# Two blocks of j per instruction in the pairwise loop of a hyperbolic graph layer: load, mask, second gelu and both vector products widened, node features read from the summing table

## The chip, the cores and the metric

One core of a Trainium2 chip. The metric is the device time of one execution, in microseconds (us). Each version is run several times in rounds with the kernel before on the same chip. Engines in the profile: PE is TensorE's matmuls, PEld its weight loads, DVE is VectorE, ACT is ScalarE, POOL is GpSimd, SP the engine that issues the loads.

## The reference, cut to what matters

There are 3327 nodes with 64 features and a dense 0/1 adjacency matrix of 3327 x 3327 (44 MB in float32).

```python
h = relu(layernorm(x))
# layer 0, hyperbolic attention; c = 1 / r**2
x_t     = logmap0(h, c)
adj_att = sigmoid((x_t @ w_l)[:, None] + (x_t @ w_r)[None, :] + b) * adj
x_local = logmap(h[:, None, :], h[None, :, :], c)        # every pair of nodes
support = einsum('ij,ijd->id', adj_att, x_local)
x = x + proj(expmap(h, support, c), c)
# layer 1: weights that decay with the rank of a neighbour in its row
h = relu(layernorm(x))
rank = cumsum(adj != 0, axis=1); ...                     # cut
x = x + w @ (h @ weight) + bias
```

For the argument it is enough that layer 0 needs for each pair (i, j) a sigmoid, a scalar function of a "distance", and their product with adj, summed over j with the features of j. Layer 1 needs how many neighbours of i lie behind j.

## The kernel before

The columns i are cut into four strips of 8, 8, 6 and 4 blocks of 128 (1024, 1024, 768 and 512 wide). Within a strip a loop runs over the 26 blocks of j, from the last to the first. This is its body, with comments added; `V` is VectorE, `A` ScalarE, `T` TensorE.

```python
for j in range(NB - 1, -1, -1):
    ad = work.tile([P, FMAX], F32, name="ad", bufs=4)
    nc.sync.dma_start(ad[:, :F], adj_t[j * P : (j + 1) * P, i0 : i0 + F])
    mask = work.tile([P, FMAX], BF16, name="mask", bufs=3)
    V.tensor_scalar(mask[:, :F], ad[:, :F], 0.0, None, op0=ALU.not_equal)        # mask
    for f0, f1 in hv:                                                            # counts, into ONE bank pc
        if not first:
            T.matmul(pc[:, f0:f1], ca, before[:, f0:f1], ...)
        T.matmul(pc[:, f0:f1], cb, mask[:, f0:f1], ...)
    before = mask
    ...                                                                          # count copy: pc -> uint8,
    if j % (2 if b0 == 0 else 4): A.activation(kept, counts, AF.Relu)            # on ScalarE
    else:                         V.tensor_scalar(kept, counts, 0.0, None, op0=ALU.max)   # or VectorE

    sg = work.tile([P, FMAX], F32, name="sg", bufs=3)
    A.activation(sg[:, :F], left_b[:, :F], AF.Tanh, bias=right[:, j : j + 1], scale=0.5)
    V.scalar_tensor_tensor(sg[:, :F], sg[:, :F], 1.0, ad[:, :F], ...)            # product "sg"

    pq = ps.tile([P, FMAX], F32, name="pq", bufs=2)
    for f0, f1 in hv:                                                            # distances
        T.matmul(pq[:, f0:f1], ju[:KB, j, :], iuf[:, f0:f1], start=True, stop=False)
        T.matmul(pq[:, f0:f1], jz[:, j, :], izf[:, f0:f1], start=False, stop=True)
    s = work.tile([P, FMAX], F32, name="s", bufs=3)
    A.activation(s[:, :F], pq[:, :F], AF.Gelu, scale=-WG / QS)                   # first gelu
    A.activation(s[:, :F], s[:, :F], AF.Gelu, scale=WH)                          # second gelu
    V.scalar_tensor_tensor(s[:, :F], s[:, :F], WD, sg[:, :F], ...)               # product "s"
    for f0, f1 in hv:                                                            # the sum, four passes
        T.matmul(po[: D + 1, f0:f1], hw[:, j, :], s[:, f0:f1], start=first, stop=last)
    next(steps, None)                  # one step of the previous strip's closing arithmetic
```

After the last block of j a VectorE copy takes `po` out; this copy marks the strip's end below. The closing arithmetic of a strip (some 70 instructions, most of them 128 x 8) is spread over the next strip's loop. A scheduler at compile time fixes each engine's order of instructions. In PSUM, where this program puts its matmul results, it keeps two `pq`, one `pc` and one `po`.

The features of a node are kept twice: as `h`, and weighted, as `hw`, the summing table.

## Time and profile before

| | before |
|---|---|
| time | 484.36 us median of 3 runs (482.84 to 486.17) |
| span of the profiled execution | 483.4 us, mean granted clock 0.946 |
| strips end at (start of the closing copy) | 145.14, 250.15, 333.19, 394.20 us |
| busy | TensorE 82%, VectorE 86%, ScalarE 75% of the span |

A page of the profile has, among others, a line for the chain of work that ended last (shares of the span by engine) and lines for the costliest groups of instructions: line, engine, operation, output and inputs, count, then busy time and mean duration in ns, then the engine's idle time just before them with what ended most of it. The page of the kernel before:

```profile
DVE 54%; PE 22%; ACT 11%; issue 8%; DMA 3%; POOL 1%; DVEq 0%; ACTq 0%; POOLq 0%
...
L831 DVE SCALAR_TENSOR_TENSOR sg<-sg,ad 128x1024 f32<-128x1024 f32 (+2 forms) x104 | 105.6, 1019 | 7.5 <-ACT sg L830 7.3
L840 DVE SCALAR_TENSOR_TENSOR s<-s,sg 128x1024 f32<-128x1024 f32 (+2 forms) x104 | 106.2, 1021 | 5.3 <-ACT s L839 5.2
```

The two products, 104 of each, are half of VectorE's work, and VectorE carries half of the chain. The view of waits over 55 to 250 us (the full part of strips 1 and 2) has for each consumer the releaser, the total in us, how often, and the longest. For the count bank `pc` the kernel before has, among others, these three:

```profile
ACT behind_hi L824 <- PE pc L819: 5.7, 3, 4.5
...
ACT behind_lo L824 <- PE pc L819: 2.1, 3, 1.5
...
PE pc L818 <- ACT behind_lo L824: 1.1, 2, 0.9
```

TensorE waits 1.1 us in all for ScalarE's count copies in nearly 200 us.

### The profile page before, as it was taken

The page shows a single profiled execution, that of the slowest core. Times are in us where ns is not written, and L with a number is a line of the kernel's source. Part 1 is how long each engine was busy: PE and PEld are TensorE (multiplying, and loading weights), DVE is VectorE, ACT ScalarE, POOL GpSimd, SP SyncE. Part 2 cuts the span into 40 slices and gives each one's busy share as a digit, 9 for nine tenths or more (in the row PEclk, how much of TensorE's full clock was granted, in tenths as well). Part 3 has the DMA queues.
Part 4 walks back from the last instruction along what each step waited for, and adds up shares of the span by engine and source line. Part 5 has one row for each costly group of instructions (what it writes and reads, how often), then busy time and mean ns, then how long its engine had stood idle before and what let it go on. Part 6 is the DMA issues. An engine that isn't in the chain of part 4 may idle for free.

```text
span 483.4 us, 4793 instructions
## 1 busy us (share of the span) xinstructions
PE 396.6 (82%) x1484; PEld 159.0 (33%) x1484; DVE 413.6 (86%) x834; ACT 363.7 (75%) x446; POOL 14.0 (3%) x30
## 2 busy tenths in 40 slices
PE   0267799999997999998988988898899859974773
PEld 0035233333323333332333444343222214432432
DVE  3893779999988899999989999999999999997110
ACT  1345989999868999999959999995999966640000
POOL 5000000000000000001000000100000100000000
PEclk9999999999999999999999999999999997997555
DMA  7102445444451445343433453442453300000010
GB/s 208 42 10 58 135 130 170 138 163 135 130 155 45 137 149 158 122 138 123 130 105 104 147 142 109 121 120 65 116 147 110 108 2 0 0 1 1 22 32 24
DMA packets 23051, 47.79 MB, mean 99 GB/s; under 512 B 8861, under 2 KB 9291, under 8 KB 23017
## 3 DMA queue, kind: packets, MB, share of 16 engines
q1 hardware_dynamic: 20730, 46.47, 33.0%
q10 hardware_dynamic: 2062, 0.87, 0.9%
q0 software_dynamic: 224, 0.07, 0.3%
q8 instruction: 13, 0.21, 0.2%
q14 instruction: 22, 0.17, 0.1%
HBM read 45.22 MB, written 0.85 MB: 95 GB/s over the span
## 4 chain that ended last, share of the span: by engine, by line
DVE 54%; PE 22%; ACT 11%; issue 8%; DMA 3%; POOL 1%; DVEq 0%; ACTq 0%; POOLq 0%
DVE s L840 12%; PE po L842 10%; DVE sg L831 9%; DVE mask L815 6%; DVE wt L879 3%; DVE wt L880 3%; PE pw L907 3%; DVE behind_lo L826 3%; ACT s L839 2%; ACT s L838 2%; PE pw L884 2%; DMA w_lr<-in_w_att 2%; PE pc L818 2%; ACT sg L830 2%; PE pc L819 2%
## 5 line engine op out<-in xcount | busy, mean ns | idle before, releaser
L842 PE MATMUL po<-s,hw 128*65 128x512 f32 (+1 forms) x364 | 168.7, 581 | 12.4 <-DVE s L840 12.0
L831 DVE SCALAR_TENSOR_TENSOR sg<-sg,ad 128x1024 f32<-128x1024 f32 (+2 forms) x104 | 105.6, 1019 | 7.5 <-ACT sg L830 7.3
L840 DVE SCALAR_TENSOR_TENSOR s<-s,sg 128x1024 f32<-128x1024 f32 (+2 forms) x104 | 106.2, 1021 | 5.3 <-ACT s L839 5.2
L830 ACT ACTIVATE sg<-left_b,right 128x1024 f32<-128x1024 f32 (+2 forms) x104 | 103.6, 1000 | 0.3 <-DVE s L840 0.2
L839 ACT ACTIVATE s<-s 128x1024 f32<-128x1024 f32 (+2 forms) x104 | 94.1, 906 | 0.2
L838 ACT ACTIVATE s<-pq 128x1024 f32<-128x1024 f32 (+2 forms) x104 | 90.0, 870 | 3.8 <-PE pq L836 3.5
L835 PE MATMUL pq<-iu,ju 71*128 71x512 f16 (+1 forms) x182 | 68.1, 375 | 11.6 <-ACT s L838 11.4
L818 PE MATMUL pc<-mask,ca 128*128 128x512 bf16 (+1 forms) x175 | 65.2, 373 | 15.1 <-DVE behind_hi L826 6.7
L842 PEld LDWEIGHTS po<-s,hw 128*65 128x65 f32 x364 | 44.2, 138 | 100.4 <-DVE s L840 50.3
L819 PE MATMUL pc<-mask,cb 128*128 128x512 bf16 (+1 forms) x182 | 66.7, 376 | 5.7 <-DVE mask L815 5.5
L836 PE MATMUL pq<-iz,jz 128*128 128x512 f16 (+1 forms) x182 | 67.4, 375 | 0.0
L815 DVE TENSOR_SCALAR mask<-ad 128x1024 bf16<-128x1024 f32 (+2 forms) x104 | 61.0, 589 | 4.8 <-PE pc L818 2.9
L884 PE MATMUL pw<-wt,s 128*128 128x512 bf16 (+1 forms) x182 | 46.8, 413 | 16.4 <-DVE wt L880 5.5
L824 ACT ACTIVATE behind_hi<-pc 128x1024 uint8<-128x1024 f32 (+2 forms) x37 | 31.9, 861 | 25.5 <-PE pc L819 25.3
L819 PEld LDWEIGHTS <-cb 128*128 128x128 bf16 x182 | 17.9, 99 | 55.7 <-issue 44.6
L884 PEld LDWEIGHTS <-s 128*128 128x128 f16 x182 | 19.9, 110 | 38.5 <-issue 19.5
L824 ACT ACTIVATE behind_lo<-pc 128x1024 uint8<-128x1024 f32 (+2 forms) x33 | 28.2, 856 | 3.8 <-PE pc L819 3.2
L836 PEld LDWEIGHTS <-jz 128*128 128x128 f16 x182 | 18.2, 100 | 33.3 <-issue 18.1
L818 PEld LDWEIGHTS <-ca 128*128 128x128 bf16 x175 | 17.5, 100 | 31.3 <-issue 20.4
L835 PEld LDWEIGHTS <-ju 71*128 71x128 f16 x182 | 18.2, 100 | 23.9 <-issue 8.6
L902 ACT COPY ow<-pw 128x512 f32<-128x512 f32 x3 | 1.8, 586 | 30.8 <-PE pw L884 30.8
L909 DVE TENSOR_TENSOR o<-pw,x_sb 128x256 f32<-128x256 f32 (+1 forms) x7 | 2.8, 406 | 21.8 <-PE pw L907 21.8
(211 smaller groups left out, 325.6 us busy)
## 6 DMA issues: line engine op xcount, KB each, us to landing
ad<-in_adj_t SPq DMA_DIRECT2D x52, 512.0 KB, 3.6
ad<-in_adj_t SPq DMA_DIRECT2D x26, 384.0 KB, 3.2
ad<-in_adj_t SPq DMA_DIRECT2D x26, 256.0 KB, 2.8
out<-o SPq DMA_DIRECT2D x6, 128.0 KB, 2.0
x_sb<-in_x ACTq DMA_DIRECT2D x1, 416.0 KB
x_sb<-in_x SPq DMA_DIRECT2D x1, 416.0 KB
iz<-jz ACTq DMA_DIRECT2D x2, 128.0 KB
iz<-jz SPq DMA_DIRECT2D x2, 128.0 KB, 3.2
```

What stands on the lines that cost most here:

```text
L815: V.tensor_scalar(mask[:, :F], ad[:, :F], 0.0, None, op0=ALU.not_equal)
L818: T.matmul(pc[:, f0:f1], ca, before[:, f0:f1], start=False, stop=True, skip_group_check=True)
L819: T.matmul(pc[:, f0:f1], cb, mask[:, f0:f1], start=False, stop=True, skip_group_check=True)
L830: A.activation(sg[:, :F], left_b[:, :F], AF.Tanh, bias=right[:, j : j + 1], scale=0.5)
L831: V.scalar_tensor_tensor(sg[:, :F], sg[:, :F], 1.0, ad[:, :F], op0=ALU.add, op1=ALU.mult)
L835: T.matmul(pq[:, f0:f1], ju[:KB, j, :], iuf[:, f0:f1], start=True, stop=False)
L836: T.matmul(pq[:, f0:f1], jz[:, j, :], izf[:, f0:f1], start=False, stop=True)
L838: A.activation(s[:, :F], pq[:, :F], AF.Gelu, scale=-WG / QS)
L839: A.activation(s[:, :F], s[:, :F], AF.Gelu, scale=WH)
L840: V.scalar_tensor_tensor(s[:, :F], s[:, :F], WD, sg[:, :F], op0=ALU.add, op1=ALU.mult)
L842: T.matmul(po[: D + 1, f0:f1], hw[:, j, :], s[:, f0:f1], start=first, stop=last)
L884: T.matmul(pw[:, f0:f1], s2[:, j].rearrange("p c d -> p (c d)"), wt[:, f0:f1].bitcast(BF16), start=j == 0, stop=j == NB - 1)
```

## The change

The intent is to pay the fixed part of four kinds of instruction once per two blocks of j. In the kernel before this part is 0.07 us of the start-to-start time of a mask (0.60 us) and of a product (1.14), and 0.09 us of a second gelu's 0.95 (which lasts 0.639 us for 512 elements and 1.067 for 1024, so that 1024 elements cost 0.856). The loop steps by pairs of blocks: one load of 1 MB instead of two of 512 KB, one mask, one product sg, one second gelu, one product s. Tanh, first gelu, counts and all matmuls stay per block. The buffers keep four blocks of `ad` (two pairs), and get four instead of three of `mask`, `sg` and `s`. The table `h` goes; the closing arithmetic reads `hw` and multiplies by the factor `unw` that undoes the weight.

```diff
-    h = const.tile([P, NB, D], F32, name="h")
...
-        V.tensor_mul(h, rl, wide(y, NB))
+        V.tensor_scalar(unw, babs, 2.0 / WA, None, op0=ALU.mult)
...
-        hs, v, xs = h[:, bs], agg[:, :, :D], x_sb[:, bs]
+        hs, v, xs = hw[:, bs, :D], agg[:, :, :D], x_sb[:, bs]
...    (three small multiplications by unw[:, bs] are added in the closing arithmetic)
-        for j in range(NB - 1, -1, -1):
...    (the body shown above)
+        for j0 in range(NB - 2, -1, -2):
+            ad = work.tile([P, 2, FMAX], F32, name="ad")
+            nc.sync.dma_start(ad[:, :, :F],
+                              adj_t[j0 * P : (j0 + 2) * P, i0 : i0 + F].rearrange("(t p) f -> p t f", p=P))
+            mask = work.tile([P, 2, FMAX], BF16, name="mask")
+            V.tensor_scalar(mask[:, :, :F], ad[:, :, :F], 0.0, None, op0=ALU.not_equal)
+
+            sg = work.tile([P, 2, FMAX], F32, name="sg")
+            s = work.tile([P, 2, FMAX], F32, name="s")
+            for t in (1, 0):
+                j = j0 + t
...    (counts and count copy of block j)
+                A.activation(sg[:, t, :F], left_b[:, :F], AF.Tanh, bias=right[:, j : j + 1], scale=0.5)
...    (distances of block j)
+                A.activation(s[:, t, :F], pq[:, :F], AF.Gelu, scale=-WG / QS)
+            V.scalar_tensor_tensor(sg[:, :, :F], sg[:, :, :F], 1.0, ad[:, :, :F], op0=ALU.add, op1=ALU.mult)
+            A.activation(s[:, :, :F], s[:, :, :F], AF.Gelu, scale=WH)
+            V.scalar_tensor_tensor(s[:, :, :F], s[:, :, :F], WD, sg[:, :, :F], op0=ALU.add, op1=ALU.mult)
+            for t in (1, 0):
+                j = j0 + t
+                for f0, f1 in hv:
+                    T.matmul(po[: D + 1, f0:f1], hw[:, j, :], s[:, t, f0:f1], start=j == NB - 1, stop=j == 0)
+                next(steps, None)
```

More of the change, by code (lines that the diff above doesn't have):

```diff
@@ L515, in wide @@
         return t[:, :, None].to_broadcast([P, n, D])
-    h = const.tile([P, NB, D], F32, name="h")
-    x2, bal, balm, nrm, left, right = (
-        const.tile([P, NB], F32, name=n) for n in ("x2", "bal", "balm", "nrm", "left", "right"))
+    x2, bal, balm, nrm, left, right, unw = (
+        const.tile([P, NB], F32, name=n) for n in ("x2", "bal", "balm", "nrm", "left", "right", "unw"))
     hw = const.tile([P, NB, D + 1], F32, name="hw")
@@ L707, in post @@
         V.tensor_reduce(xy, dt, AX.X, ALU.add)
+        V.tensor_mul(xy, xy, unw[:, bs])
         V.scalar_tensor_tensor(sa, xy, m2c, agg[:, :, D], op0=ALU.mult, op1=ALU.add)
@@ L712, in post @@
         yield
-        V.tensor_mul(w, hs, wide(sa, nb))
+        V.tensor_mul(k, sa, unw[:, bs])
+        V.tensor_mul(w, hs, wide(k, nb))
         yield
@@ L747, in post @@
         yield
+        V.tensor_mul(t0, t0, unw[:, bs])
         V.tensor_mul(w, hs, wide(t0, nb))
@@ L809, in fast @@
         before = None
-        for j in range(NB - 1, -1, -1):
-            first, last = j == NB - 1, j == 0
-            ad = work.tile([P, FMAX], F32, name="ad", bufs=4)
-            nc.sync.dma_start(ad[:, :F], adj_t[j * P : (j + 1) * P, i0 : i0 + F])
-            mask = work.tile([P, FMAX], BF16, name="mask", bufs=3)
-            V.tensor_scalar(mask[:, :F], ad[:, :F], 0.0, None, op0=ALU.not_equal)
-            for f0, f1 in hv:
-                if not first:
-                    T.matmul(pc[:, f0:f1], ca, before[:, f0:f1], start=False, stop=True, skip_group_check=True)
-                T.matmul(pc[:, f0:f1], cb, mask[:, f0:f1], start=False, stop=True, skip_group_check=True)
-            before = mask
-            kept = behind(j)[:, i0 : i0 + F].rearrange("p (k q t) -> p k t q", t=2, q=P)
-            counts = pc[:, :F].rearrange("p (k t q) -> p k t q", t=2, q=P)
-            if j % (2 if b0 == 0 else 4):
-                A.activation(kept, counts, AF.Relu)
-            else:
-                V.tensor_scalar(kept, counts, 0.0, None, op0=ALU.max)
-            sg = work.tile([P, FMAX], F32, name="sg", bufs=3)
-            A.activation(sg[:, :F], left_b[:, :F], AF.Tanh, bias=right[:, j : j + 1], scale=0.5)
-            V.scalar_tensor_tensor(sg[:, :F], sg[:, :F], 1.0, ad[:, :F], op0=ALU.add, op1=ALU.mult)
-            pq = ps.tile([P, FMAX], F32, name="pq", bufs=2)
-            for f0, f1 in hv:
-                T.matmul(pq[:, f0:f1], ju[:KB, j, :], iuf[:, f0:f1], start=True, stop=False)
-                T.matmul(pq[:, f0:f1], jz[:, j, :], izf[:, f0:f1], start=False, stop=True)
-            s = work.tile([P, FMAX], F32, name="s", bufs=3)
-            A.activation(s[:, :F], pq[:, :F], AF.Gelu, scale=-WG / QS)
-            A.activation(s[:, :F], s[:, :F], AF.Gelu, scale=WH)
-            V.scalar_tensor_tensor(s[:, :F], s[:, :F], WD, sg[:, :F], op0=ALU.add, op1=ALU.mult)
-            for f0, f1 in hv:
-                T.matmul(po[: D + 1, f0:f1], hw[:, j, :], s[:, f0:f1], start=first, stop=last)
-            next(steps, None)
@@ new lines, in fast @@
+        for j0 in range(NB - 2, -1, -2):
[9 more added lines that the diff above has]
+                for f0, f1 in hv:
+                    if before is not None:
+                        T.matmul(pc[:, f0:f1], ca, before[:, f0:f1], start=False, stop=True, skip_group_check=True)
+                    T.matmul(pc[:, f0:f1], cb, mask[:, t, f0:f1], start=False, stop=True, skip_group_check=True)
+                before = mask[:, t]
+                kept = behind(j)[:, i0 : i0 + F].rearrange("p (k q t) -> p k t q", t=2, q=P)
+                counts = pc[:, :F].rearrange("p (k t q) -> p k t q", t=2, q=P)
+                if j % (2 if b0 == 0 else 4):
+                    A.activation(kept, counts, AF.Relu)
+                else:
+                    V.tensor_scalar(kept, counts, 0.0, None, op0=ALU.max)
+                A.activation(sg[:, t, :F], left_b[:, :F], AF.Tanh, bias=right[:, j : j + 1], scale=0.5)
+                pq = ps.tile([P, FMAX], F32, name="pq", bufs=2)
+                for f0, f1 in hv:
+                    T.matmul(pq[:, f0:f1], ju[:KB, j, :], iuf[:, f0:f1], start=True, stop=False)
+                    T.matmul(pq[:, f0:f1], jz[:, j, :], izf[:, f0:f1], start=False, stop=True)
+                A.activation(s[:, t, :F], pq[:, :F], AF.Gelu, scale=-WG / QS)
[4 more added lines that the diff above has]
+                j = j0 + t
+                for f0, f1 in hv:
+                    T.matmul(po[: D + 1, f0:f1], hw[:, j, :], s[:, t, f0:f1], start=j == NB - 1, stop=j == 0)
+                next(steps, None)
@@ L844, in fast @@
         for _ in steps:
             pass
-        ot = work.tile([P, FMAX], F32, name="s", bufs=3)[: D + 1]
+        ot = work.tile([P, 2, FMAX], F32, name="s")[: D + 1, 0]
         V.tensor_copy(ot[:, :F], po[: D + 1, :F])
```

## The prediction

> **What bounds the kernel now.** I read the stages first. The copy that closes each column strip (line L848) starts at 145.14, 250.15, 333.19 and 394.20 us, so I cut the span near those times and asked for the busy time of each engine in each stretch. The columns are the stretch, its length, then busy time and instruction count of PE, PEld, DVE, ACT and POOL, then the clock, the DMA share and GB/s.
> ```profile
> 48.00:146.00 98.00, 92.40 (x293) 32.20 (x291) 88.70 (x89) 87.56 (x91) 0.00 (x0) 1.00 0.47 143
> 146.00:251.00 105.00, 97.47 (x330) 34.79 (x331) 101.35 (x176) 97.66 (x106) 2.19 (x1) 0.98 0.43 128
> 251.00:332.00 81.00, 72.15 (x319) 33.25 (x319) 78.81 (x166) 76.38 (x105) 2.39 (x1) 1.00 0.42 118
> 332.00:395.00 63.00, 53.67 (x171) 16.41 (x170) 60.28 (x169) 55.37 (x105) 1.73 (x1) 1.00 0.35 95
> ```
> The first strip is bound by nothing alone: TensorE 94% of it, VectorE 91%, ScalarE 89%. In strips 2 to 4 VectorE is the fullest (97%, 97%, 96%), because it also does the previous strip's closing arithmetic. Before 48 us is a preamble that is a chain of small steps, after 395 us a tail that the change hardly touches. DMA is under half busy everywhere.
>
> Next I read the timeline for what one instruction really costs in a full queue. In the lines below the first number is the start, the second the duration.
> ```profile
> 240.62 1.21 DVE L840 SCALAR_TENSOR_TENSOR s<-s,sg 128x1024 f32<-128x1024 f32 x1
> 241.76 1.21 DVE L831 SCALAR_TENSOR_TENSOR sg<-sg,ad 128x1024 f32<-128x1024 f32 x1
> 242.90 0.68 DVE L815 TENSOR_SCALAR mask<-ad 128x1024 bf16<-128x1024 f32 x1
> 243.50 1.21 DVE L831 SCALAR_TENSOR_TENSOR sg<-sg,ad 128x1024 f32<-128x1024 f32 x1
> ```
> The durations overlap: from start to start a product takes 1.14 us and a mask 0.60 us. By form, the product at 128x512 lasts 0.684 us and at 128x1024 1.217 us, so 512 elements cost 0.533 us, and 1024 cost 1.066 us. The fixed part that merging can remove is therefore 1.14 - 1.066 = 0.07 us per instruction, not the 0.15 us that the durations suggest. The mask gives the same 0.07 (0.60 less half of 1.066).
>
> ScalarE and TensorE in the same way:
> ```profile
> 149.94 1.03 ACT L838 ACTIVATE s<-pq 128x1024 f32<-128x1024 f32 x1
> 150.85 1.15 ACT L830 ACTIVATE sg<-left_b,right 128x1024 f32<-128x1024 f32 x1
> 151.89 1.06 ACT L839 ACTIVATE s<-s 128x1024 f32<-128x1024 f32 x1
> 152.84 1.15 ACT L830 ACTIVATE sg<-left_b,right 128x1024 f32<-128x1024 f32 x1
> ```
> ```profile
> 83.03 1.88 PE L842 MATMUL po<-s,hw 128*65 128x512 f32 x4
> 84.74 0.38 PE L818 MATMUL pc<-mask,ca 128*128 128x512 bf16 x1
> 84.96 0.38 PE L819 MATMUL pc<-mask,cb 128*128 128x512 bf16 x1
> ```
> First gelu 0.91 us, tanh 1.04, second gelu 0.95; a count copy on ScalarE 0.90. TensorE needs 1.71 us for the sum of one block of j (four passes) and eight matmuls of 0.216 us for counts and distances, 3.44 us per block of j.
>
> So in strip 1, per block of j: TensorE 3.44; VectorE 0.60 + 2 x 1.14 + half a count copy 0.57 = 3.45; ScalarE 1.04 + 0.91 + 0.95 + 0.45 = 3.35. The three are within 3%.
>
> [...]
> ```profile
> 154.95 0.40 PE L835 MATMUL pq<-iu,ju 71*128 71x512 f16 x1 [2.04 <-ACT s L838]
> 155.16 3.57 PE L842 MATMUL po<-s,hw 128*65 128x512 f32 x4
> ```
> The four passes that took 1.88 us above take 3.57 here, after 2.04 us without work.
>
> **The change part by part.**
> Loop, VectorE: in each of 52 pairs, three merged instructions (mask, sg, s) save 0.07 each: 52 x 3 x 0.07 = 10.9 us of its queue, 2.7 per strip. ScalarE: one merged gelu saves 0.09: 4.8 us, 1.2 per strip. TensorE: the same matmuls, nothing saved. "Both products" means the two vector products; the matmuls stay per block.
> Closing arithmetic: three small multiplications more per strip, 0.08 us each where neighbours are independent: +0.25 per strip, up to +0.5 in the tail where it stands alone.
> Preamble: the table h disappears, an instruction in a queue that has no gap between 13.5 and 37 us:
> ```profile
> 22.34 1.88 DVE L646 TENSOR_TENSOR h<-rl,y 128x1664 f32<-128x1664 f32 x1
> ```
> It steps by 1.80; unw costs 0.1: -1.7 us. In the compiled order the first gelu now comes before the first tanh, so one of two table loads falls away, -1.28:
> ```profile
> 46.28 1.28 ACT L830 ACT_TABLE_LOAD   x1
> 48.74 1.28 ACT L838 ACT_TABLE_LOAD   x1
> ```
> The pipe's start: in the compiled order the first pair on ScalarE is gelu, tanh, tanh, gelu, tanh, wide gelu: 0.91 + 1.04 + 1.04 + 0.91 + 1.04 + 1.80 = 6.7, then a wide product of 2.20. From left_b to the first sum matmul that is 1.28 + 6.7 + 2.2 + 0.1 = 10.3 us, against 55.23 - 46.26 = 9.0 now. So the preamble's 3.0 us shrink to 1.7, and half of that waits behind TensorE.
> Strip 1: per pair TensorE 6.88, VectorE 6.68 (1.14 + 2.20 + 2.20 + 1.14), ScalarE 6.6. The lower two get lower, but the top one stays, and 26 x 3.44 = 89.4 us already fill the time from the first sum matmul to the end of the strip (55.2 to 145.1). Gain 0; I allow +0.5 for coarser hand-overs.
> Strips 2 to 4: the 2.7 - 0.25 = 2.4 us would be whole gains if VectorE stayed full. But each strip drains and fills. At its end, the last pair's sum takes 3.4 us after the last product instead of 1.7; at its start, the first s needs two tanh, two gelu, a wide gelu (6 to 6.7 us after left_b instead of 3 to 4). Closing arithmetic, a mask and a count copy fill part of it, and I put the extra idle time of VectorE at 2.0, 1.7 and 1.2 us in strips 2, 3 and 4 (as widths fall). Net -0.4, -0.7, -1.2. Tail +0.4.
> Loads: ad keeps four blocks, now as two buffers. Time to landing was 2.8, 3.2 and 3.6 us for 256, 384 and 512 KB, 0.8 us per 256 KB, so a 1 MB load takes about 5.2 (estimate); the next buffer is asked for one pair earlier, 6.7 us in strip 1. Hidden, with 1.5 us to spare.
> Sum: -1.7 + 0.5 - 0.4 - 0.7 - 1.2 + 0.4 = -3.1 us. From 484.4 that is 481.3; I say 481.
>
> **The rivals.**
> A. VectorE is the bound throughout and fill costs nothing: -10.9 - 3.0 + 1.2 = -12.7 us, 471.7. For it: VectorE has the largest share of the chain that ended last (54%) and 97% of strips 2 to 4. Against: strip 1, where TensorE's matmuls are unchanged, and ScalarE and TensorE at 93% of strip 2.
> B. Coarser hand-overs cost more than I allow: TensorE waits for a whole pair, runs into gaps over 2 us and pays half rate (1.7 us each time, from the lines above), four times or more; mask buffers wait. Then +5 to +10: 489 to 494. For it: only two pq buffers and one count bank, so TensorE cannot run far ahead.
> C. The 1 MB loads land late[...]: VectorE waits up to 1 us before each mask, +10 us or more in strip 1 alone. Against: DMA share 0.47. Unlikely.
>
> **Range and chances.** A and B pull in opposite directions from 481, and A is the more likely of the two in strips 3 and 4. 472 to 492 spans nearly the whole of A and most of B. Faster by over 2% (under 474.7) needs three quarters of A: 0.17. Slower by over 2% (over 494) needs B with C: 0.10. Within: 0.73.
>
> **What would show it.** Right: wide products step by about 2.20, masks 1.14, wide gelu 1.80; VectorE's busy sum falls by more than the span does, as idle time before s and sg (releaser ScalarE) grows at the strips' starts; strip 1 lasts as long as now; two, not three, table loads between 39 and 50 us. Wrong: if strip 1 gets shorter by over 3 us, TensorE was not its bound; if the waits of mask name the load of ad, it is C; if many sums take 3.4 us or more per four passes, it is B.

## The result

| | before | after |
|---|---|---|
| time, median | 484.96 us (482.84 to 486.17, 4 runs) | 497.38 us (495.50 to 498.53, 4 runs) |
| ratio | | 1.0257, 95% interval 1.0206 to 1.0308: slower |
| span, clock of the profiled execution | 483.4 us, 0.946 | 493.8 us, 0.921 |
| start to end of strip 1 (closing copy starts) | 145.14 | 145.74 (+0.6) |
| strip 2, from copy to copy | 105.01 | 112.37 (+7.4) |
| strip 3 | 83.04 | 84.81 (+1.8) |
| strip 4 | 61.01 | 60.20 (-0.8) |
| from there to the end | 89.2 | 90.7 (+1.5) |

A ratio here is the mean time of one kernel's fast runs over the mean of the other's in the same rounds, so not quite the ratio of the medians. All experiments below give it against the kernel before.

The busy time of the changed kernel by strip (stretch, length, then busy time and count of PE, PEld, DVE, ACT, POOL, then clock, DMA share, GB/s), cut near its own strip ends:

```profile
48.00:146.00 98.00, 89.58 (x283) 31.86 (x286) 85.97 (x51) 83.82 (x75) 0.00 (x0) 0.97 0.43 143
146.00:258.00 112.00, 98.55 (x329) 36.52 (x334) 100.47 (x139) 97.12 (x93) 2.19 (x1) 0.97 0.36 119
258.00:343.00 85.00, 74.07 (x319) 34.96 (x323) 79.64 (x129) 73.79 (x90) 1.93 (x1) 0.98 0.37 115
343.00:403.00 60.00, 52.12 (x162) 17.50 (x165) 56.81 (x125) 54.10 (x92) 1.91 (x1) 0.97 0.33 97
```

Read the second line against the one that the prediction shows. Strip 2 took seven microseconds more, and the busy time of VectorE (101.35 before, 100.47 now), ScalarE (97.66, 97.12) and TensorE (97.47, 98.55) is the same within about one. No engine works longer; all three stand idle more. That excludes "an engine became the bound" at once.

Next the page of the changed kernel, with the lines that answer to those of before:

```profile
DVE 37%; PE 31%; ACT 20%; issue 7%; DMA 3%; POOL 1%; DVEq 0%; ACTq 0%; POOLq 0%
...
L843 DVE SCALAR_TENSOR_TENSOR s<-s,sg 128x2048 f32<-128x2048 f32 (+2 forms) x52 | 98.0, 1884 | 6.8 <-ACT s L842 6.6
...
L817 DVE TENSOR_SCALAR mask<-ad 128x2048 bf16<-128x2048 f32 (+2 forms) x52 | 53.0, 1019 | 3.0 <-DMA ad<-in_adj_t 1.9
...
ad<-in_adj_t SPq DMA_DIRECT2D x26, 1024.0 KB, 5.0
```

The chain that ended last is now spread over three engines (37%, 31% and 20%), where VectorE alone had half of it (54%). The masks wait 1.9 us in all for loads, and a 1 MB load lands 5.0 us after its issue, so the loads are nearly hidden.

The waits over 55 to 250 us for the count bank, in the changed kernel:

```profile
ACT behind_hi L831 <- PE pc L826: 12.0, 6, 7.1
...
PE pc L825 <- ACT behind_lo L831: 6.2, 5, 3.1
ACT behind_lo L831 <- PE pc L826: 5.8, 4, 2.4
...
PE pc L825 <- ACT behind_hi L831: 2.3, 3, 1.3
```

ScalarE waits 12.0 + 5.8 = 17.8 us for counts, where it was 5.7 + 2.1 = 7.8 (one wait at the end of strip 1 is 7.1 of it, and was 4.5); TensorE waits 6.2 + 2.3 = 8.5 us for ScalarE's count copies, where it was 1.1. How such a stretch looks is in the timeline of the changed kernel near the end of strip 2 (start, duration, engine, line, operation; in brackets the idle time before it and its releaser):

```profile
236.90 3.63 PE L847 MATMUL po<-s,hw 128*65 128x512 f32 x8
...
241.43 1.03 ACT L831 ACTIVATE behind_lo<-pc 128x1024 uint8<-128x1024 f32 x1 [1.62 <-PE pc L826]
...
244.15 1.92 ACT L842 ACTIVATE s<-s 128x2048 f32<-128x2048 f32 x1
...
246.46 1.05 ACT L831 ACTIVATE behind_lo<-pc 128x1024 uint8<-128x1024 f32 x1
...
247.56 0.38 PE L825 MATMUL pc<-mask,ca 128*128 128x512 bf16 x1 [3.11 <-ACT behind_lo L831]
...
248.45 5.33 PE L847 MATMUL po<-s,hw 128*65 128x512 f32 x8
...
258.11 1.22 DVE L853 COPY s<-po 65x1024 f32<-65x1024 f32 x1 [4.91 <-PE po L847]
```

TensorE runs the sums of both blocks in one lump of eight passes. ScalarE stands for 1.62 us, since the next counts are behind that lump in TensorE's order. Then the roles change: the next count copy stands behind the wide gelu (and a cast) in ScalarE's order, and TensorE stands for 3.11 us. The lump after that gap takes 5.33 instead of 3.63 us (the granted clock was 0.50 from 248.45 to 251.86 us), and VectorE waits 4.91 us for the end of the last sum, where before it waited 0.48.

### The profile page after: what moved, and what is told of

Its sections match the earlier page's. It is cut to its first block, busy times and chain, and to the rows that moved or that the text cites. A ratio compares the mean times of both kernels' runs of the same rounds, so it can differ in the third digit from the quotient of the medians.

```text
span 493.8 us, 4436 instructions
## 1 busy us (share of the span) xinstructions
PE 395.5 (80%) x1460; PEld 163.5 (33%) x1484; DVE 408.5 (83%) x690; ACT 357.4 (72%) x393; POOL 13.7 (3%) x30
## 4 chain that ended last, share of the span: by engine, by line
DVE 37%; PE 31%; ACT 20%; issue 7%; DMA 3%; POOL 1%; DVEq 0%; ACTq 0%; POOLq 0%
PE po L847 16%; DVE s L843 6%; DVE sg L841 5%; ACT s L840 5%; ACT sg L835 5%; ACT s L842 4%; DVE mask L817 4%; DVE wt L884 3%; DVE wt L885 3%; PE pw L912 3%; PE pc L825 2%; PE pw L889 2%; PE pc L826 2%; PE pq L838 2%; DMA w_lr<-in_w_att 2%
## 5 line engine op out<-in xcount | busy, mean ns | idle before, releaser
L847 PE MATMUL po<-s,hw 128*65 128x512 f32 (+1 forms) x364 | 162.1, 585 | 7.0 <-DVE s L843 6.5
L841 DVE SCALAR_TENSOR_TENSOR sg<-sg,ad 128x2048 f32<-128x2048 f32 (+2 forms) x52 | 99.3, 1913 | 12.6 <-ACT sg L835 12.6
L843 DVE SCALAR_TENSOR_TENSOR s<-s,sg 128x2048 f32<-128x2048 f32 (+2 forms) x52 | 98.0, 1884 | 6.8 <-ACT s L842 6.6
L835 ACT ACTIVATE sg<-left_b,right 128x1024 f32<-128x1024 f32 (+2 forms) x104 | 102.5, 1003 | 1.1 <-DVE s L843 1.1
L840 ACT ACTIVATE s<-pq 128x1024 f32<-128x1024 f32 (+2 forms) x104 | 88.5, 872 | 4.4 <-PE pq L839 2.3
L842 ACT ACTIVATE s<-s 128x2048 f32<-128x2048 f32 (+2 forms) x52 | 83.5, 1606 | 0.1
L847 PEld LDWEIGHTS po<-s,hw 128*65 128x65 f32 x364 | 49.4, 142 | 97.9 <-issue 70.1
L826 PE MATMUL pc<-mask,cb 128*128 128x512 bf16 (+1 forms) x164 | 59.8, 374 | 6.4 <-DVE mask L817 6.3
L817 DVE TENSOR_SCALAR mask<-ad 128x2048 bf16<-128x2048 f32 (+2 forms) x52 | 53.0, 1019 | 3.0 <-DMA ad<-in_adj_t 1.9
L826 PEld LDWEIGHTS <-cb 128*128 128x128 bf16 x182 | 17.6, 98 | 62.2 <-issue 51.2
```

The costliest lines, as they stand in the source:

```text
L817: V.tensor_scalar(mask[:, :, :F], ad[:, :, :F], 0.0, None, op0=ALU.not_equal)
L826: T.matmul(pc[:, f0:f1], cb, mask[:, t, f0:f1], start=False, stop=True, skip_group_check=True)
L835: A.activation(sg[:, t, :F], left_b[:, :F], AF.Tanh, bias=right[:, j : j + 1], scale=0.5)
L840: A.activation(s[:, t, :F], pq[:, :F], AF.Gelu, scale=-WG / QS)
L841: V.scalar_tensor_tensor(sg[:, :, :F], sg[:, :, :F], 1.0, ad[:, :, :F], op0=ALU.add, op1=ALU.mult)
L842: A.activation(s[:, :, :F], s[:, :, :F], AF.Gelu, scale=WH)
```

## The experiments

Eighteen kernels ran. The table has them all. "To copy 1" is the time of strip 1's closing copy; strips 2 to 4 are from copy to copy; all times are in us.

| run | what it is | median | ratio (95%) | to copy 1 | strip 2 | strip 3 | strip 4 |
|---|---|---|---|---|---|---|---|
| before | | 484.4 | 1 | 145.1 | 105.0 | 83.0 | 61.0 |
| after | the whole change | 497.4 | 1.026 (1.021 to 1.031) | 145.7 | 112.4 | 84.8 | 60.2 |
| feat_only | only `h` removed | 482.4 | 0.996 (0.993 to 0.999) | 141.6 | 105.0 | 83.2 | 61.2 |
| keep_h | only the wide loop | 496.3 | 1.024 (1.022 to 1.027) | 148.0 | 111.1 | 84.8 | 60.5 |
| load_mask | after, but sg, gelu and s per block | 478.3 | 0.989 (0.985 to 0.994) | 139.5 | 104.0 | 82.4 | 60.3 |
| load_only | load_mask, but mask per block too | 484.9 | 1.004 (1.000 to 1.009) | 141.5 | 106.0 | 83.7 | 61.7 |
| ends_fine | after, per block in each strip's first and last pair | 492.5 | 1.015 (1.010 to 1.019) | 145.4 | 111.6 | 85.5 | 58.7 |
| gelu_wide | load_mask + wide second gelu | 485.9 | 1.001 (0.998 to 1.004) | 142.3 | 110.6 | 83.5 | 59.7 |
| sg_wide | load_mask + wide sg | 488.9 | 1.010 (1.002 to 1.018) | 143.6 | 109.7 | 83.6 | 62.1 |
| s_wide | load_mask + wide s | 495.3 | 1.022 (1.019 to 1.025) | 150.0 | 108.5 | 83.3 | 61.1 |
| both_products | load_mask + wide sg and s | 495.3 | 1.022 (1.019 to 1.024) | 150.2 | 107.7 | 83.3 | 61.6 |
| wide_narrow | load_mask in strips 1, 2; after in 3, 4 | 480.8 | 0.993 (0.989 to 0.997) | 141.0 | 103.6 | 83.9 | 60.4 |
| wide_1pass | after, sum in one pass | 487.0 | 1.009 (1.000 to 1.017) | 139.9 | 110.1 | 80.8 | 61.8 |
| fine_1pass | load_mask, sum in one pass | 481.7 | 0.998 (0.993 to 1.003) | 137.4 | 105.7 | 81.9 | 61.8 |
| ad3 | after, third load buffer | 494.0 | 1.018 (1.014 to 1.021) | 151.5 | 105.4 | 86.1 | 59.0 |
| ad3_fine | load_mask, third load buffer | 479.7 | 0.992 (0.987 to 0.996) | 141.2 | 106.2 | 82.2 | 58.8 |
| after_s3 | after, third s buffer | 492.2 | 1.017 (1.013 to 1.020) | 145.2 | 111.2 | 84.1 | 59.1 |
| spread_sums | after, sums not in a lump | 496.8 | 1.027 (1.022 to 1.032) | 149.5 | 110.1 | 84.1 | 62.8 |
| wide_nopc | after, no wait for the count bank (wrong result) | 492.0 | 1.017 (1.012 to 1.022) | 146.8 | 108.5 | 86.1 | 59.7 |
| fine_nopc | load_mask, the same (wrong result) | 484.2 | 1.000 (0.996 to 1.003) | 143.2 | 106.2 | 84.2 | 60.3 |

All others gave the right result. One warning holds for all: the compiled order of every engine is made anew for each source, so a variant differs from its neighbour by more than its edit. How much that is worth will come out below. The runs were also taken in several groups, on different chips, each group with the kernel before beside it. The text below takes differences of medians; by the ratios they come out up to 2 us smaller or 1 us larger (the changed kernel against load_mask: 19.1 us by medians, 17.6 by ratios, and 18.0 for keep_h, which ran in one group with load_mask). "Fine" means load_mask's loop.

### The two halves apart: feat_only and keep_h

feat_only is the kernel before with the `h` and `unw` lines of the diff alone; keep_h has the loop of the diff alone.

```diff
 # feat_only                                   # keep_h
-        V.tensor_mul(h, rl, wide(y, NB))       (the loop's hunk of the diff, h stays)
+        V.tensor_scalar(unw, babs, 2.0 / WA, None, op0=ALU.mult)
...
```

> Only the second half of the change: no table h, the closing arithmetic reads the summing table hw through the factor unw; the loop is that of the kernel before. Theory G (the coarse hand-over of pairs at the strips' starts and ends costs the time; the features are nearly free): 483 to 485.5 us, first sum matmul some 1.5 us earlier, tail up to 0.5 us longer. Rival F (the feature half and the order it brings cost a good part): 488 or more, with the tail (from the last strip's copy to the end) 1 us or more longer, as in the changed kernel (90.7 against 89.2 us).

> Only the first half: the loop over two blocks of j per instruction, with the table h kept. Theory G: 495 to 500 us, second strip (copy to copy) about 112 us against 105 before. Rival F: 490 or less.

The features alone gain 0.4%, and the wide loop alone loses 2.4%: the loss is the loop's. The gain is more than the removed instruction. In feat_only the first sum of strip 1 starts at 50.70 us, before at 55.23 us:

```profile
50.70 3.68 PE L844 MATMUL po<-s,hw 128*65 128x512 f32 x4 [2.60 <-DVE s L842]
```

In the changed kernel it starts at 55.97 us again:

```profile
55.97 2.54 PE L847 MATMUL po<-s,hw 128*65 128x512 f32 x4
```

From the first sum to the copy strip 1 takes 89.9 us before (145.14 - 55.23), 90.9 in feat_only and 89.8 in the changed kernel. In these three, strip 1 is TensorE's from its first sum on (the prediction counts 89.4 us of matmuls), and its time is set by when that comes. It is not so in every variant: in ends_fine, s_wide, both_products and ad3 the same stretch takes 94.0 to 94.7 us. The features make it come 4.5 us earlier, and the wait for a whole pair spends 5.3 us.

### Which part of the loop: load_mask and load_only

```diff
 # load_mask: inside "for t in (1, 0)", per block
+                V.scalar_tensor_tensor(sg[:, t, :F], ...)   # behind the tanh
+                A.activation(s[:, t, :F], s[:, t, :F], AF.Gelu, scale=WH)
+                V.scalar_tensor_tensor(s[:, t, :F], ...)    # and the sum of block j
 # load_only: the mask as well (and the products s and the sums written behind both blocks)
+                V.tensor_scalar(mask[:, t, :F], ad[:, t, :F], 0.0, None, op0=ALU.not_equal)
```

> The changed kernel with load and mask over two blocks, but both vector products, the second gelu and the sum per block again (tiles stay two blocks wide, two buffers). Theory G: the hand-over from s to the sum is fine again, so most of the loss goes: 482 to 488 us, second strip 103 to 107 us. Rival L (the 1 MB loads into only two buffers, and the tiles of two blocks held until both are used, cost the time): 493 or more, with waits of mask for the load of ad and waits of tanh for s growing.

> Only the load and the tiles are two blocks wide; mask and everything else per block. The mask's 52 merges were worth 52 x 0.07 = 3.6 us of VectorE's queue: 480 to 483 us if that and the features make up load_mask's gain; 478 or less if the gain came from the order or the buffers.

This is the cleanest comparison. load_mask has the same tiles, buffers and loads as the changed kernel; only the three instructions and the sums go per block. It is 19 us faster than the changed kernel (478.3 against 497.4) and 1.1% faster than the kernel before, better than I expected, and **no version here was faster**. So neither the 1 MB loads nor buffers that come free in pairs cost the time by themselves. load_only is 6.7 us slower than load_mask, where the merged mask should be worth 52 x 0.07 = 3.6 us. Its edit also writes the products s and the sums behind both blocks, so it is not the mask alone: a first sign that the order, in the source or as compiled, moves some microseconds by itself.

### Only at the strips' ends? ends_fine

```diff
+                fine = j0 in (0, NB - 2)      # per block in the first and last pair
```

> The changed kernel, with products, second gelu and sum per block in the first and last pair of each strip only, 8 of 52 pairs. Theory G: from the second strip's copy to its first sum matmul and from the last product to the closing copy are as before again (10 and 2 us against 14.4 and 4.9), so the second strip is about 107 us and the whole 486 to 490. Rival M (the pairs in the middle of the strips cost it as well, since the three engines hand over in larger lumps): 493 or more, second strip 110 or more.

If filling and draining were all, this would be near load_mask. It brings back 5 of 19 us and falls between the ranges that I had given to the two theories. The first sum of strip 2 does come 9.6 us after the copy (154.95 against 145.39) instead of 14.35 us (160.09 against 145.74 in the changed kernel), but the first wide pair loses it again, at the load. The timeline of VectorE in ends_fine:

```profile
162.46 1.23 DVE L817 TENSOR_SCALAR mask<-ad 128x2048 bf16<-128x2048 f32 x1 [3.69 <-DMA ad<-in_adj_t]
```

This load could be issued only at 156.06 us, when both products sg of the first pair had been done. Nor did the edit give the strip's end back: from the last product s to the copy strip 2 takes 4.8 us here, 4.9 in the changed kernel and 2.1 before, since the sums of the last two pairs still run one behind the other (16 passes from 248.55 us on). So the run shows that this edit does not cure the loss. It does not clear the strips' ends of it; more on them in the section on the prediction.

### The load's two buffers: ad3 and ad3_fine

```diff
-            ad = work.tile([P, 2, FMAX], F32, name="ad")
+            ad = work.tile([P, 2, FMAX], F32, name="ad", bufs=3)
-        agg = post_pool.tile([P, 8, D + 1], F32, name="agg", bufs=2)    # to make room
+        agg = post_pool.tile([P, 8, D + 1], F32, name="agg", bufs=1)
```

> The changed kernel with a third adjacency buffer of two blocks (room made by one instead of two agg buffers, which one strip later are long free). Theory P (the lumps of two blocks in the in-order queues cost the time: sums of four products of 0.86 us come bunched, TensorE waits for count copies that stand behind a wide gelu): the waits of mask for the load (about 2 us in all) go, 494 to 498 us. Rival L (loads that may start only when a whole pair is let go): 490 or less.

> The best version so far (load and mask over two blocks, everything else per block, 478.3) with a third buffer for the loads and one instead of two for the gathered sums. If VectorE still waits for loads there, 474 to 477; if not, within 1.5 us of 478.3.

On the wide loop a third load buffer brings back 3.4 us; on the fine loop nothing (479.7 against 478.3). In ad3 strip 2 falls to 105.4, as long as before, while strip 1 grows from 145.7 to 151.5, with no cause in the edit that I can name other than another compiled order. VectorE's waits for loads between 55 and 250 us were 1.4 us in the changed kernel, and ad3 has none over 0.2 us, so the waits themselves are a small part of the loss. Whether the buffer or the order gave strip 2 its 7 us back stays open.

### One instruction at a time: gelu_wide, sg_wide, s_wide, both_products

```diff
 # e.g. s_wide, against load_mask: the product s behind "for t", over both blocks, then both sums
+            V.scalar_tensor_tensor(s[:, :, :F], s[:, :, :F], WD, sg[:, :, :F], op0=ALU.add, op1=ALU.mult)
```

> Load, mask and second gelu over two blocks; both vector products per block. Theory P says that the wide gelu (1.80 us, with the count copies behind it in ScalarE's queue and both s products behind it in time) is a main lump: 486 to 492 us, against 478.3 with load and mask alone. Rival S (the wide products, s above all, are the lump): 476 to 482.

> Load, mask and the s product over two blocks; second gelu and sg product per block. Rival S: the sums of a pair become ready together and run as eight passes, so TensorE's other work waits: 486 to 492 us. Theory P: the s product of 2.2 us alone costs less than the gelu: 479 to 485.

> Load, mask, sg and s products over two blocks, only the second gelu per block. If the lumps add up, this is the changed kernel less the gelu's part: Theory P 481 to 487 us; rival S 489 to 496.

> Load, mask and the sg product over two blocks; second gelu and s product per block. both_products was as slow as s_wide alone, so the sg product should be free: 476 to 481 us by theory T (nothing on TensorE waits for sg). Rival Q: a lump of 2.2 us in VectorE's queue costs as much here as in s_wide: 487 or more.

Each widening alone loses against load_mask: the gelu 7.6 us, sg 10.6, s 17.0; sg and s together 17.0; all three 19.1 (by the ratios 5.7, 10.2, 15.9, 15.6 and 17.6). s_wide came out above both of my ranges. The losses do not add up, as waits don't when one covers another. sg_wide, whose sums are written per block, came out where I had expected it only if the lump of sums was not needed for a loss. In its trace, though, part of them are in lumps all the same: between 56 us and strip 2's copy, 12 runs of eight passes beside 25 of four (load_mask: 2 and 46). And by strips the losses are nearly all in strips 1 and 2.

### Only where the engines are balanced? wide_narrow

```diff
+                fine = b0 < 16                 # strips 1 and 2 per block
```

> Load and mask over two blocks everywhere; sg, second gelu, s and sum per block in strips 1 and 2 (1024 wide), over two blocks in strips 3 and 4 (768 and 512 wide). If the loss sits only where the three engines are balanced, strips 3 and 4 cost what they cost in the changed kernel (84.8 and 60.2) and strips 1 and 2 what they cost with load and mask alone (139.5 and 104.0): 480.5. If the wide instructions of strip 2 and 1 hurt what follows, strip 3 falls to 82.4 or less: 476 to 478. Over 485: neither, and the compiled order alone is worth that much.

Widening only in strips 3 and 4 costs 2.5 us of median over load_mask, and 1.7 by the ratios ((0.9928 - 0.9893) x 484); strip 3 takes 83.9 instead of 82.4, strip 4 the same. So the loss lies in the 1024-wide strips 1 and 2. In strip 1 TensorE has 3.44, VectorE 3.45 and ScalarE 3.35 us of work per block; that this balance is the reason, and not the width itself, the run does not show.

### Slack for one engine: wide_1pass and fine_1pass

Here `s` and a copy of `hw` are float16, so that the sum takes half as many passes (182 in all instead of 364), and TensorE falls well under the other two. The passes are also shorter: the sum of a pair in wide_1pass is four passes in 0.86 us from start to start (76.33 to 77.19 us), against eight in 3.44 (the four passes of a block took 1.71). The 1.7 us per pair that I expected below was an estimate, half of 3.44. The closing copy of a strip also gets a buffer of its own instead of one of `s`.

```diff
-            s = work.tile([P, 2, FMAX], F32, name="s")
+            s = work.tile([P, 2, FMAX], F16, name="s")
+        G.tensor_copy(hw16, hw)
-    T.matmul(po[: D + 1, f0:f1], hw[:, j, :], s[:, t, f0:f1], ...)
+    T.matmul(po[: D + 1, f0:f1], hw16[:, j, :], s[:, t, f0:f1], ...)
```

> The changed kernel with s and a copy of the summing table in 16 bits, so that the sum takes one pass on TensorE instead of two (1.7 us per pair and 1024 columns instead of 3.44, TensorE some 2.6 us per block of j instead of 3.44; the output is less exact on purpose). To be read against fine_1pass. Theory T (in the wide strips TensorE has no slack, so the later start of each sum behind a wide s product is lost for good): with slack on TensorE most of the distance of 19 us between the changed kernel and load_mask goes, and wide_1pass is within 6 us of fine_1pass; some 470 us. Rival Q (wide products hold up VectorE's and ScalarE's own queues, whatever TensorE has to do): still 12 us or more slower than fine_1pass.

> load_mask with the same 16-bit s and table: TensorE has slack, VectorE is the bound with the same instructions as in load_mask. Both theories: 462 to 476 us; it is the yardstick for wide_1pass.

TensorE's busy time between 55 and 250 us falls from 177.0 to 136.3 us in the wide loop and from 183.7 to 139.3 in the fine one. The distance of wide and fine falls from 19.1 to 5.3 us: **coarse hand-overs were cheap here when TensorE had room, and dear when none of the three engines had**. What the cheaper sum did not do is make the fine loop faster (481.7 against 478.3, where I had expected 462 to 476): there VectorE was busy for 186.5 of 195 us with or without it, and the granted clock fell to 0.86 (load_mask: 0.94; between 55 and 250 us 0.93 against 1.00), so the matmuls that are left ran at half rate more often (they start 0.43 us apart near 203 us, 0.22 near 197).

### The lump in TensorE's order? spread_sums

The sum of a pair is written two pairs later, and edges in the compiled order put its first block between the distances of the later pair's blocks.

```diff
+                if old is not None:            # the pair before last
+                    mm = add(old, t)           # sum of its block t
+                    behind_of(near, mm)        # ordered behind the distances of block j
```

> The changed kernel with all its two-block instructions; only the sums on TensorE move: the sum of a pair is written two pairs later, and edges in the compiled order put its first block between the distances of that later pair's first and second block, its second block behind them. So TensorE never meets eight sum passes (3.4 us) in a lump. Theory L (the lump in TensorE's in-order queue is what starves ScalarE of distances in strips 1 and 2): strip 2 falls from 112.4 to 107 or less and the whole to 485 to 490. Rival C (the lump is not the cause; the two-pair hand-over of s and sg between VectorE and ScalarE is): 494 to 499, strip 2 within 2 us of the changed kernel's. The later sums lengthen each strip's end by up to 2 us, which is in both figures.

The timeline of TensorE shows that the edit did what it should: runs of two and four passes with other matmuls between.

```profile
199.26 1.88 PE L822 MATMUL po<-s,hw 128*65 128x512 f32 x4
...
202.67 1.07 PE L822 MATMUL po<-s,hw 128*65 128x512 f32 x2 [0.67 <-DVE s L866]
```

It brought nothing: 496.8, ratio 1.027. TensorE's idle time between 55 and 250 us falls from 18.0 to 15.0, and VectorE's rises from 15.7 to 19.3. But the edit also made waits that were not there:

```profile
ACT s L863 <- PE po L822: 6.5, 8, 1.6
```

There are two pair buffers of `s`, so a pair's first gelu now waits until the late sums have let one go (6.5 us, 0.3 in the changed kernel), and the tanh waits 4.8 us for products s (1.1 in the changed kernel). So spreading the sums in this way gains nothing; that the lump is not a cause is not shown, since what the edit gave back may have gone into the new waits.

### The one count bank? wide_nopc and fine_nopc

Both give a wrong result: the count copies read the mask instead of the count bank, in the same sizes on the same engines, so that TensorE and ScalarE no longer wait for each other there.

```diff
-                counts = pc[:, :F].rearrange("p (k t q) -> p k t q", t=2, q=P)
+                counts = mask[:, t, :F].rearrange("p (k t q) -> p k t q", t=2, q=P)
```

> Gives a wrong result on purpose: the changed kernel, but the count copies read the mask instead of the count bank, with the same sizes and engines, so no engine waits for the one count bank any more; all matmuls stay. In the changed kernel ScalarE waited 17.8 us for counts and TensorE 8.5 us for count copies between 55 and 250 us, against 7.8 and 1.1 us before. Theory N (the single count bank, handed to and fro twice per pair between TensorE and ScalarE, is where coarser steps lose the time): the distance between this and fine_nopc is 8 us or less of total time, and this is 484 to 490. Rival: the distance stays at 14 to 20 us, because the waits only move to the other hand-overs.

> Gives a wrong result on purpose: the kernel with load and mask over two blocks and everything else per block (478.3), with the count copies reading the mask instead of the count bank. It had few waits on counts (TensorE 2.5 us, ScalarE 10.8 us, of which 9.1 at the two strips' ends): 474 to 479.

The waits of wide_nopc over 55 to 250 us:

```profile
DVE s L843 <- ACT s L842: 10.4, 8, 1.7
PE pq L838 <- ACT s L840: 9.6, 11, 2.7
```

The waits for the count bank are gone, and in their place VectorE waits longer for the second gelu (6.2 us in the changed kernel, 10.4 here) and TensorE for a free distance bank (5.3, 9.6). The total gains 5.4 us, to 492.0, which misses the 484 to 490 that I had given for "the count bank is the cause". The distance from wide to fine is 7.8 us, within the 8 that I had given for it, but that is not sound: most of the fall from 19 comes from fine_nopc, which was expected at 474 to 479 and is 5.9 us slower than load_mask though it has fewer waits to make. (Its TensorE was busy at half rate for 16.4 us between strip 1's first sum and strip 4's copy, load_mask's for 3.1.) So this pair shows that the waits move, and that a variant can come out 6 us slower with nothing in its edit to explain it. It does not show the bank as the cause.

### Room for s: after_s3

```diff
-            s = work.tile([P, 2, FMAX], F32, name="s")
+            s = work.tile([P, 2, FMAX], F32, name="s", bufs=3)     # agg with one buffer, as above
```

> The changed kernel with three instead of two pair buffers for s (and one instead of two for the gathered sums, to make room). If the longer time from first gelu to last sum of a pair makes ScalarE wait for a free s buffer, 488 to 493 (as far as the third load buffer brought it, or more). The waits of the changed kernel's trace name free buffers of s and sg with under 1.5 us in all between 55 and 250 us, so I expect 495 to 499, no change.

492.2, so 5 us are back, against the 495 to 499 that I expected: the waits that name the free `s` buffer were under 1.5 us, so the third buffer helps somewhere upstream of them, or the order does.

## Why the prediction was wrong

481.0 us was predicted, with 472 to 492; 497.38 was measured. Step by step:

- **Durations and steps: right.** Wide products last 2.28 us and step by 2.20 (predicted 2.20), the wide mask lasts 1.22 and steps by 1.14 (1.14), the wide gelu 1.92 (step predicted 1.80: 51.45 to 53.25 us). The 1 MB load lands in 5.0 us (estimate 5.2). Table loads between 38 and 47 us: two of 1.28 us (predicted two). ScalarE's busy time fell by 6.3 us (363.7 to 357.4), against 4.8 + 1.28 predicted.
- **VectorE's saving of 10.9 us: mis-sized.** Its busy time fell by 5.1 us only (413.6 to 408.5), though `h` is gone too. In strip 2 the large instructions did save about the 2.7 us predicted (the products and masks take 74.9 us from start to start before, 72.3 after), but the 72 small ones of the closing arithmetic, which took 0.097 us each from start to start, are 75 now and take 0.117: 1.8 us more. The VectorE timeline of the changed kernel shows why:

```profile
242.90 0.17 DVE L510 TENSOR_TENSOR rs_t<-rn 128x8 f32<-128x8 f32 x1
243.10 0.17 DVE L511 TENSOR_TENSOR rs_t<-rs_t,rs_g 128x8 f32<-128x8 f32 x1
243.31 0.17 DVE L512 SCALAR_TENSOR_TENSOR rn<-rs_t,rn 128x8 f32<-128x8 f32 x1
```

With half as many large instructions to stand between, small ones come in rows more often (43 of the 75 are followed by another small one, before 22 of the 72). Where each reads what the one before wrote, as here, they start 0.20 us apart, instead of the 0.08 that the prediction took for independent neighbours and that the same trace shows for them (L511 and L702 at 242.51 and 242.59 us).
- **The preamble and strip 1: right in kind, 1.8 us off.** Predicted -1.7 and +0.5, so -1.2; measured +0.6. The first sum came 10.8 us after the table load began (55.97 - 45.21; predicted 10.3), and from there strip 1 took 89.8 us (predicted 89.4): TensorE was its bound.
- **Strip 2: the step that failed.** Predicted -0.4, measured +7.4, and with strip 3 (-0.7, +1.8) it is most of the miss. The term was "the extra idle time of VectorE at 2.0 us in strip 2", put there for the strip's drain and fill. The sum was -2.4 us of work and +2.0 of idle time; measured were -0.6 (101.36 to 100.73 us busy from copy to copy) and +8.0 (3.65 to 11.63 us idle). Cut at the first sum and at the end of the last product s, the strip's three parts show where:

| strip 2 | copy to first sum | to the end of the last product s | to the next copy |
|---|---|---|---|
| before: time, of it VectorE idle | 10.0, 1.2 us | 92.9, 2.0 | 2.1, 0.5 |
| after | 14.4, 2.6 | 93.1, 4.1 | 4.9, 4.9 |

So the fill and the drain that the term was for were under-sized: 5.9 us more idle time at the two ends, the drain alone 4.4 where I had allowed 1.7. And 2.1 us came in the middle, where I had let the hand-overs be free. The middle should even have become shorter, since the first sum now comes with a pair done and not a block (some 3.7 us, an estimate: 92.9 us for 25 blocks). In strips 3 and 4 it did (73.2 to 70.7 and 53.0 to 49.0 us), which made up for a fill that was 2.6 and 2.3 us longer there; in strip 2 it did not. Which hand-over kept it from that stays open.
- **Strip 4: right** (-1.2, measured -0.8). **Tail:** +0.4, measured +1.5.
- **Rival A** (VectorE the bound, 471.7) was wrong. Even load_mask, the best version, gained only half of what A claimed (6 of 12.7 us).
- **Rival B** (coarser hand-overs) had the mechanism, and I put its total at 489 to 494 and slower by over 2% at 0.10. What I gave for its price was half rate on TensorE, four or more times 1.7 us, and that part came near. The views of two of the stretches at half rate, before and after (the third figure from the end is the granted clock, 0.50):

```profile
155.17:158.58 3.41, 3.41 (x6) 0.85 (x6) 3.08 (x4) 3.41 (x4) 0.00 (x0) 0.50 0.70 225
248.45:251.86 3.41, 3.41 (x5) 0.98 (x5) 3.41 (x4) 1.91 (x1) 0.00 (x0) 0.50 0.00 0
```

What sets half rate off these traces do not show. It came after 2.04 us without work before and after 3.11 us in the changed kernel, but in wide_nopc a gap of 2.66 us (before 251.52 us) was followed by full rate, 3.65 us for eight passes. Nor was TensorE idle in the whole 3.41 us before the two stretches above: it was busy for 1.37 and 0.89 us of them. Between strip 1's first sum and strip 4's copy TensorE was busy at half rate for 3.4 us before, for 15.0 us after (in five stretches) and for 3.1 us in load_mask. At a granted clock of 0.50 half of that is time lost, an estimate: 1.7, 7.5 and 1.5 us. So half rate itself can be at most 5.8 of the 12.4 us, and it does not go with the loss from variant to variant: s_wide has 13.2 us of it and loses 17.0 us against load_mask, gelu_wide has 23.1 and loses 7.6. The rest is waiting, for which B had allowed too little; and it took no late loads (C) to pass 494.
- **Rival C** (late loads) was wrong as the cause, as far as the waits show it: 1.9 us of them, and 3.4 us from a third buffer.

What is shown: the loss lies in the wide instructions sg, gelu and s and not in loads, mask, buffers or features (load_mask against the changed kernel, 19 us); the kernels with the product s wide in all strips and the sums in float32 lie at 492 to 497 us, and those with all three per block at 478 to 485, so no order that came up here bridges the two. The product s alone causes nearly all of the loss and sg alone a part; the gelu's 7.6 us (5.7 by the ratios) is no more than what orders move. The loss lies in strips 1 and 2 (wide_narrow), and it falls to 5 us when TensorE is given room (the one-pass pair). A reading that fits all of this, argued and not shown, is that with three engines equally loaded nothing but the buffers takes up the wait for a whole pair, at a strip's start and end above all, and there are few: two distance banks, one count bank, two pairs of `s`, `sg` and `ad`. Each bit of room that was given back went with part of the time (a third load buffer 3.4 us, a third `s` buffer 5.2, no count bank 5.4, per-block ends 4.9), but each of these is under the 6 us of the next paragraph, so none is shown to be a cause.

What stays open: how the loss divides among the hand-overs and between a strip's ends and its middle, and why the wide s alone costs nearly as much as all. Each variant came with a new compiled order, and in load_only, fine_nopc and ad3 some 6 us of a whole or of a strip moved without a cause in the edit. Differences under that are not to be put down to an edit.

## What to carry to other kernels

Measure what merging can save from start to start in a full queue, not from durations (0.07 us here and not 0.15), and then ask what waits for the merged instruction: here three engines were loaded alike, and VectorE, which had been 97% full in strip 2, did 0.6 us less work there and stood idle 8.0 us longer, at the strip's start and end and in part between. Merge what only feeds ahead, as load and mask here (1.1% faster than before, which another order could also have brought), and leave per block what another engine is waiting for. And where a scheduler makes the order, try the parts apart; the whole change hid a version that was 19 us faster.
